# Where a two-layer kernel computes inverse norms and rates: in the preparation instead of at the head of each recurrence piece

## The chip, the cores and the metric

The kernel runs on one core of one Trainium2 chip. The metric is the device time of one execution in microseconds (us). Three runs of the kernel before gave 3310.29, 3290.19 and 3306.56 us, with a median of 3306.56. A core has five engines that each work through their own list of instructions in order: TensorE (PE, matrix products; PEld is its loading of weights), VectorE (DVE), ScalarE (ACT, activation functions), GpSimd (POOL) and SyncE (SP), which here issues the transfers (DMA).

## The reference, cut to what matters

The input is `hidden_states` of shape (16, 512, 256): 16 sequences of 512 tokens with 256 channels, which are 16 heads of 16. Two layers follow, each with an attention part and a feed-forward part; all are residual, with scale and shift from a conditioning vector. The change lies in the attention part of the first layer, whose "fast weights" are a recurrence over chunks of 16 tokens:

```python
q = l2norm(silu(short_conv(h @ Wq.T, cq)).reshape(b, l, H, HD))
k = l2norm(silu(short_conv(h @ Wk.T, ck)).reshape(b, l, H, HD))
v =        silu(short_conv(h @ Wv.T, cv)).reshape(b, l, H, HD)
lr = softplus(h @ Wlr.T + BASE_LR).reshape(b, l, H, 2)
# per chunk: scores of k and q with W_in (4 x 16 per head), softmaxes,
# outer products with v and k that update W_in and W_out, outputs o_t
o = layernorm over the 16 channels of a head; o * (h @ Wg.T) @ Wo.T
```

`l2norm` divides each head's 16 channels by their Euclidean norm, so for every token and head one number, the inverse norm, has to be found for q and one for k. `lr` holds two rates per token and head. The first layer's feed-forward part is a low-rank one with gelu; the second layer has attention over a window of 64 tokens plus four global ones, and a channel mix with gates. The window attention adds masks to its scores.

## The kernel before, in words

**Units.** The sequences are split in two halves of eight, and the tokens in eight blocks of 64. One half and one block make a unit; there are 16. Each unit goes through five streams, written as Python generators: `prepare` (projections, convolution and silu of q, k and v; gate), `chain` (the recurrence), `mlp`, `attend` (window attention), and `mix`. `timetable` (L1111) gives each stream's steps times in units, and the loop at L1126 records the steps of all units sorted by these times. A scheduler then orders each engine's instructions by its own estimate of when each becomes ready. Units of the same half follow one another in the recurrence; units of different halves are independent, so two recurrence chains run side by side.

**Two layouts.** `prepare` has channels on partitions (128 of the 256 channels in each of two tiles, 512 columns = 8 sequences x 64 tokens). The recurrence has sequence and head on partitions (8 x 16 = 128) and, in a piece of 32 tokens, 16 channels x 32 tokens in a row. Between them the data go through device memory: `prepare` writes q, k, v and lr (L422, L461), and `load_piece` (L553) reads a piece back in the other layout (L559, L561). A unit has two pieces (`NPC` = 2), a piece two chunks.

**What is done at the head of a piece.** `load_piece` loads k, v, q and lr into buffers of which each half has one. It then makes the rates: ACT adds 0.001 (L562) and takes the three steps of `log_sigmoid_tail` (L201 to L203), DVE puts them together (L565). For k and then q, ACT squares the 128x512 piece (L550, into one of five buffers shared with the big products), DVE sums the 16 channels (`ss`, L571), ACT takes the inverse root as exp(-0.5 ln x) (L196, L197), and POOL multiplies the piece (L573). ACT then copies a chunk into `tok` with tokens ahead of channels (L589), and DVE makes the first scores from it (L519, L520).

**What is done at the end of a piece.** `finish_piece` (L657) takes the layer norm over a head's channels: mean (L665), squares `osq` (L550), their sum `ov` (L670), its inverse root (L196, L197), product (L673); the result is stored (L674). It works in q's buffer, so the next piece's q can be loaded only after that store.

**Buffers of the preparation.** `t2k("a", ...)` gives 128x512 fp32 buffers from a ring of three (`RING`, L118): `y` (a silu result), `lrT`, `gsb`. `bank` gives one of three banks of the matmuls' accumulator memory (L111), which the streams share. silu needs another function table than ln and exp; `run` (L213) keeps its activations together between two table loads.

**Masks.** All 12 masks (three kinds of block, two parities, two orientations; 128 columns each, bf16) lie on chip, and `add_mask` (L859) adds two of them to a bank by a matmul with the identity (L862). Kinds 0, 1 and 2 belong to blocks 0, 1 and all later ones.

Of the kernel before, what the change touches and what calls it, by code (L numbers as in the profile page):

```python
# [10 lines left out]
F32 = mybir.dt.float32  # L11
# [57 lines left out]
def parity_scales():  # L69

    ch = np.arange(P)
    even = (ch // D) % 2 == 0
    s = 1.0 / math.sqrt(D)
    group, slot = ch // 32, ch % 32
    part = slot // NS < NPART
    sel = -((slot[:, None] % NS == np.arange(NS)[None, :]) & part[:, None]).astype(np.float32)
    k2, pair, _ = np.unravel_index(np.arange(32), (2, 4, NGLOB))  # L80
    selg = np.stack(
        [(group[:, None] == pair) & (slot[:, None] % NS == 2 * k2 + e) & part[:, None] for e in range(2)], 1
    ).astype(np.float32)
    ones_g = np.tile(np.arange(8)[None, :] == (4 * k2 + pair)[:, None], (NR, 1))
    parts = [
        np.stack([even * s, ~even * s, even, ~even], 1),
        group[:, None] == np.arange(4)[None, :],
        sel,
        -selg.reshape(P, -1),
        ones_g,  # L90
    ]
    return np.ascontiguousarray(np.concatenate([p.astype(np.float32) for p in parts], 1))

# [2 lines left out]
def adaln_blocks(ctx: ExitStack, tc: tile.TileContext, a: dict, out: bass.AP):  # L96
# [18 lines left out]
        return ps_a.tile([P, 512], F32, tag="abank", name=name)  # L115


    RING = dict(a=3, b=3, c=6, d=2)  # L118

    def t2k(stream, name, shape=None):  # L120
        return work.tile(shape or [P, 512], F32, tag=f"t2k_{stream}", name=name, bufs=RING[stream])
# [51 lines left out]
    mu = plain("mu", [P, 2, 2])  # L173
    mu1 = ctile([P, 2, 2], "mu1")
    nc.vector.tensor_scalar(mu1, mu, -1.0, 1.0, mul, add)
    marks = plain("parity", [P, 8 + NS + 2 * 32 + 8])
    parity, rowgrp = marks[:, :4], marks[:, 4:8]
    ones_g = marks[:, 72 + NS :]
    ones = ctile([P, 32], "ones")
    nc.vector.memset(ones, 1.0)  # L180
    ones_bf = const.tile([NPART, P], BF16, tag="ones_bf", name="ones_bf")
# [1 line left out]
    sel_bf = const.tile([P, NS + 64], BF16, tag="sel_bf", name="sel_bf")  # L183
    nc.vector.tensor_copy(sel_bf, marks[:, 8 : 72 + NS])
    sel, selg = sel_bf[:, :NS], sel_bf[:, NS:].rearrange("p (n k) -> p n k", n=2)
    masks = const.tile([P, 12, P], BF16, tag="masks", name="masks")
    ident_bf = const.tile([P, P], BF16, tag="ident_bf", name="ident_bf")
    nc.vector.tensor_copy(ident_bf, ident)

# [49 lines left out]
    with tc.tile_pool(name="mod", bufs=1) as mp:  # L239
        masks_f = mp.tile([P, 12, P], F32, tag="masks_f", name="masks_f")  # L240
        nc.sync.dma_start(masks_f, a["masks"].rearrange("p (n k) -> p n k", n=12))
        nc.vector.tensor_copy(masks, masks_f)
        b2_row = mp.tile([1, C], F32, tag="b2_row", name="b2_row")
        nc.sync.dma_start(b2_row, a["V2b"][RANK:])
        b2_parts = mp.tile([1, NPART, C], BF16, tag="b2_parts", name="b2_parts")
# [157 lines left out]
    def prepare(u):  # L403
# [3 lines left out]
        for pc in range(NPC):  # L407
            for n in "qkvo":
                spill(f"{n}{u}_{pc}", [HB, H, D, PT])
            spill(f"lr{u}_{pc}", [HB, H, 2, PT])  # L410
        x = load_x(u, f"xa{u}", "xa", 1)
        hT = hidden("a", f"hTa{u}")
        yield from norm_T(x, 0, 0, b0, f"a{u}", hT)
# [3 lines left out]
        for k in range(2):  # L417
            nc.tensor.matmul(pp[: 2 * H, :], lhsT=w_lr[:, k, :], rhs=hf[k], start=k == 0, stop=k == 1)
        lrT = t2k("a", f"lrT{u}", [P, HB, TB])[: 2 * H]
        nc.scalar.copy(lrT.rearrange("p b t -> p (b t)"), pp[: 2 * H, :])  # L420
        for pc in range(NPC):
            nc.sync.dma_start(  # L422
                spilled[f"lr{u}_{pc}"].rearrange("b h j t -> (h j) b t"),
                lrT[:, :, pc * PT : (pc + 1) * PT],
            )

        for n in range(3):
            ys, convs = [], []
# [30 lines left out]
            for k2, (y, _) in enumerate(ys):  # L459
                for pc in range(NPC):  # L460
                    nc.sync.dma_start(  # L461
                        spilled[f"{'qkv'[n]}{u}_{pc}"][:, k2 * H // 2 : (k2 + 1) * H // 2].rearrange(
                            "b h d t -> (h d) b t"
                        ),
                        y[:, :, pc * PT : (pc + 1) * PT],
                    )
            yield

# [84 lines left out]
    def load_piece(u, pc):  # L553
        half = place(u)[0]
        tag = f"{u}_{pc}"
        s = {}
        for n in "kvq":
            s[n] = rec.tile([P, D, PT], F32, tag=f"dt_{n}_{half}", name=f"dt_{n}{tag}", bufs=1)
            nc.sync.dma_start(s[n], spilled[f"{n}{u}_{pc}"].rearrange("b h d t -> (b h) d t"))  # L559
        lr = rec.tile([P, 2, PT], F32, tag=f"lr_{half}", name=f"lr{tag}", bufs=1)  # L560
        nc.sync.dma_start(lr, spilled[f"lr{u}_{pc}"].rearrange("b h j t -> (b h) j t"))  # L561
        nc.scalar.activation(lr, lr, AF.Copy, bias=0.001)  # L562
        tmp = small(half, f"lrt{tag}", 2 * PT).rearrange("p (j t) -> p j t", j=2)
        log_sigmoid_tail(lr, tmp)
        nc.vector.scalar_tensor_tensor(lr, lr, 0.0, tmp, ALU.max, add)  # L565
        s["lr"] = lr
        s["sum"] = small(half, f"qs{tag}", PT)
        for n in "kq":
            sq = squares(half, s[n], f"sq_{n}{tag}")
            ss = small(half, f"ss_{n}{tag}", PT)  # L570
            nc.vector.tensor_reduce(ss, sq, AX.X, add)  # L571
            inverse_root(ss)
            nc.gpsimd.tensor_tensor(s[n], s[n], over_d(ss), mul)  # L573
        return s


# [185 lines left out]
    def window_attention(i, x):  # L762
# [94 lines left out]
            return keys[:, k2, r, 2 * e : 2 * e + 2].rearrange("p s t -> p (s t)")  # L857

        def add_mask(dst, query_first):  # L859
            at = 2 * min(tb, 2) + (0 if query_first else 6)  # L860
            m = masks[:, at : at + 2].unsqueeze(1).to_broadcast([P, 2, 2, P])
            nc.tensor.matmul(dst, lhsT=ident_bf, rhs=m, start=False, stop=True, skip_group_check=True)  # L862

# [1 line left out]
            nc.tensor.matmul(dst, lhsT=lhsT, rhs=rhs, start=start, stop=False, skip_group_check=True)  # L865

        slots = [(s, s // 2, s % 2) for s in range(NS)]
        queries = lambda r: lambda k2, e: qs[:, k2, 2 * r + e].rearrange("p h t -> p (h t)")

        def find_maxima(r):  # L870
# [313 lines left out]
```

## Time and profile before

| | PE | DVE | ACT | POOL |
|---|---|---|---|---|
| busy, us | 2424.1 | 2396.2 | 1762.1 | 1669.3 |
| share of the span | 73% | 73% | 53% | 51% |
| instructions | 16784 | 4513 | 3738 | 1575 |

The profiled execution took 3303.97 us, and its span from first to last instruction is 3302.2 us. The granted TensorE clock was 0.78 on average. Transfers moved 186.42 MB, 56 GB/s over the span.

Instructions that the change touches, each with its count and the mean of one:

| line, engine | what | count | mean, ns |
|---|---|---|---|
| L550 ACT | squares of k, of q | 32, 32 | 1073, 1069 |
| L571 DVE | sums ss_k, ss_q | 32, 32 | 681, 680 |
| L565 DVE | rates put together | 32 | 376 |
| L573 POOL | k, q times inverse norm | 32, 32 | 1270, 1268 |
| L418 PE | rates projected, 32 columns by 512 | 64 | 739 |
| L862 PE | masks added | 512 | 447, 431 |

A row of the profile reads: line, engine, operation, output<-inputs by the program's names, shapes and count, then busy time, the mean of one, and the idle time of the engine just before, with what ended it. In the views ordered by time a row begins with start and duration in us, and ends, in brackets, with the idle time before it and its releaser. A row that stands for several instructions ends with x and their number. In the busy table by stage the columns are the stretch, its length, busy time (and instructions) of PE, PEld, DVE, ACT and POOL, the granted clock, the busy share of the DMA engines and GB/s. "Share of the chain" is the share of the chain of waits that ended last.

### The profile page before, as it was taken

How to read it: one execution, taken by the hardware profiler on the slowest of the kernel's cores; microseconds unless marked ns; L12 is line 12 of the kernel's file. 1: busy time of each engine (PE TensorE's matmuls, PEld its weight loads, DVE VectorE, ACT ScalarE, POOL GpSimd, SP SyncE). 2: the span in 40 equal slices, each digit the busy share in tenths (PEclk: the TensorE clock that was granted, in tenths of full speed). 3: DMA queues.
4: the chain of work that ended last, by engine and by line, in shares of the span. 5: the costliest groups of instructions: out<-in, count | busy, mean ns of one | idle time of the engine just before them, and what ended most of it. 6: DMA issues, size and time to landing. Idle time of an engine off the chain costs nothing.

```text
span 3302.2 us, 46348 instructions
## 1 busy us (share of the span) xinstructions
PE 2424.1 (73%) x16784; PEld 1461.5 (44%) x16784; DVE 2396.2 (73%) x4513; ACT 1762.1 (53%) x3738; POOL 1669.3 (51%) x1575
## 2 busy tenths in 40 slices
PE   3541255777787878788887878788797878878886
PEld 2210123444444445454554445454454455545564
DVE  1678787868887787788778877877878877774221
ACT  1662354556655656565655656565665645444443
POOL 0245555556566655545546555555556556543112
PEclk7675576878787877878778788788878786869887
DMA  5321112032314131231304122131403121212010
GB/s 149 78 62 19 45 40 67 24 72 56 81 33 96 30 83 46 59 78 43 81 21 100 30 70 67 43 88 37 91 17 95 28 71 34 59 35 58 15 29 27
DMA packets 439305, 186.42 MB, mean 56 GB/s; under 512 B 323937, under 2 KB 413090, under 8 KB 439074
## 3 DMA queue, kind: packets, MB, share of 16 engines
q1 hardware_dynamic: 439074, 183.44, 22.8%
q8 instruction: 132, 2.16, 0.3%
q14 instruction: 99, 0.81, 0.1%
HBM read 116.66 MB, written 66.72 MB: 56 GB/s over the span
## 4 chain that ended last, share of the span: by engine, by line
DVE 32%; PE 28%; POOL 18%; ACT 11%; issue 7%; DMA 3%; SPq 1%; POOLq 0%; DVEq 0%; ACTq 0%
POOL pd_o L526 4%; POOL pd_i L526 4%; DVE pd_kv L623 4%; DVE pp L452 3%; DVE sc_v L519 3%; PE ph L728 3%; PE py L865 3%; PE st L865 2%; PE pz L865 2%; DVE sv L520 2%; PE pproj L994 2%; POOL pd_kv L526 2%; DVE mx L881 2%; DVE do L628 2%; PE pka L1031 2%
## 5 line engine op out<-in xcount | busy, mean ns | idle before, releaser
L526 POOL TENSOR_TENSOR pd_o<-e_k,dt_v 128x1024 f32<-128x1024 f32 x128 | 299.0, 2343 | 234.4 <-DVE e_k L541 234.2
L865 PE MATMUL st<-qs,keys 32*128 32x128 f32 x2048 | 234.3, 351 | 107.2 <-DVE mx L881 47.8
L526 POOL TENSOR_TENSOR pd_i<-e_v,dt_k 128x1024 f32<-128x1024 f32 x128 | 297.3, 2354 | 21.4 <-DVE e_v L541 21.1
L865 PEld LDWEIGHTS st<-qs,keys 32*128 32x128 f32 x2048 | 199.5, 240 | 163.0 <-DVE mx L881 61.5
L653 POOL TENSOR_TENSOR pd_kv<-hid,pd_kv 128x1024 f32<-128x1024 f32 x64 | 150.7, 2354 | 188.8 <-DVE fw L624 183.1
L628 DVE TENSOR_REDUCE do<-pd_o 128x64 f32<-128x1024 f32 x126 | 152.5, 1214 | 100.3 <-POOL pd_o L526 100.3
L628 DVE TENSOR_REDUCE di<-pd_i 128x64 f32<-128x1024 f32 x128 | 155.3, 1213 | 85.7 <-POOL pd_i L526 85.7
L865 PE MATMUL sc<-keys,qs 32*128 32x128 f32 x2048 | 169.5, 321 | 63.0 <-DVE mx L881 43.4
L700 PE MATMUL pwo<-w_WoT,oT 128*128 128x256 f32 x256 | 103.1, 560 | 142.6 <-POOL oT L693 140.7
L865 PEld LDWEIGHTS sc<-keys,qs 32*128 32x128 f32 x2048 | 134.6, 210 | 129.8 <-DVE mx L881 63.4
L881 DVE TENSOR_REDUCE mx<-sc 128x4 f32<-128x512 f32 x256 | 168.4, 679 | 19.0 <-PE sc L862 19.0
L623 DVE TENSOR_TENSOR_SCAN pd_kv<-within,pd_kv 128x1024 f32<-128x1024 bf16 x64 | 176.5, 2758 | 1.0
L526 POOL TENSOR_TENSOR pd_kv<-hid,dt_v 128x1024 f32<-128x1024 f32 x64 | 150.1, 2345 | 45.9 <-DVE hid L615 41.0
L519 DVE TENSOR_TENSOR sc_k<-tok,fw 128x1024 f32<-128x1024 f32 x128 | 155.5, 1215 | 16.0 <-ACT tok L589 14.6
L994 PE MATMUL pproj<-w_proj,yT 128*128 128x256 f32 x512 | 136.7, 411 | 36.7 <-DVE yT L972 33.7
L217 ACT ACT_TABLE_LOAD x110 | 141.1, 1283 | 19.7 <-PE pQ L735 18.1
L519 DVE TENSOR_TENSOR sc_v<-tok,fw 128x1024 f32<-128x1024 f32 x128 | 150.4, 1215 | 1.4
L865 PE MATMUL py<-pT,values 128*32 128x128 f32 x2048 | 130.4, 374 | 26.8 <-ACT pT L918 26.3
L520 DVE TENSOR_REDUCE sv<-sc_v 128x64 f32<-128x1024 f32 x128 | 149.7, 1210 | 0.0
L972 DVE TENSOR_TENSOR yT<-py,rs 128x256 f32<-128x256 f32 x128 | 51.5, 415 | 133.8 <-ACT rs L968 133.7
L918 ACT ACTIVATE pT<-st 128x512 f32<-128x512 f32 x256 | 135.4, 615 | 22.0 <-PE st L862 21.8
L865 PE MATMUL py<-pg,vglob 32*32 32x128 f32 x1536 | 71.8, 342 | 99.1 <-ACT pg L929 99.1
(244 smaller groups left out, 6821.5 us busy)
## 6 DMA issues: line engine op xcount, KB each, us to landing
values<-values SPq DMA_DIRECT2D x56, 256.0 KB
gate_a<-gates SPq DMA_DIRECT2D x64, 128.0 KB
xa<-in_x_dram SPq DMA_DIRECT2D x32, 256.0 KB
x<-in_x_dram SPq DMA_DIRECT2D x32, 256.0 KB
gate_c<-gates SPq DMA_DIRECT2D x64, 128.0 KB
gate_d<-gates SPq DMA_DIRECT2D x64, 128.0 KB
q<-y SPq DMA_DIRECT2D x64, 128.0 KB
dt_q<-q SPq DMA_DIRECT2D x32, 256.0 KB
```

Source lines behind the costliest of these rows:

```text
L217: ins = nc.scalar.activation(*args[0], **args[1])
L519: engine.tensor_tensor(pr, tok.unsqueeze(1).to_broadcast(every), w.unsqueeze(2).to_broadcast(every), mul)
L520: nc.vector.tensor_reduce(dst, pr, AX.X, add)
L526: engine.tensor_tensor(pr, hid.unsqueeze(2).to_broadcast(every), tok.unsqueeze(1).to_broadcast(every), mul)
L623: nc.vector.tensor_tensor_scan(flat, within, flat, 0.0, mul, add)
L628: nc.vector.tensor_reduce(t, pr, AX.X, add)
L653: nc.gpsimd.tensor_tensor(po, qh.unsqueeze(2).to_broadcast([P, R, D, CH]), upto, mul)
L700: nc.tensor.matmul(po[:, n * C : (n + 1) * C], lhsT=pair(oT, k, 2 * b2 + n), rhs=w_o[:, k, :], start=k == 0, stop=k == 1,)
L865: nc.tensor.matmul(dst, lhsT=lhsT, rhs=rhs, start=start, stop=False, skip_group_check=True)
L881: nc.vector.tensor_reduce(mx[:, j], sc[j].rearrange("p (s k) -> p s k", s=NS), AX.X, ALU.max)
L918: nc.scalar.activation(pT[j], st[j], AF.Exp)
L994: nc.tensor.matmul(po[:, n * C : (n + 1) * C], lhsT=yT[:, k2, par].rearrange("p e t -> p (e t)"), rhs=w_proj[:, k2, par, :], start=k2 == 0 ...
```

## The change

The inverse norms and the rates are made by `prepare`, with channels on partitions, once per unit:

- For q and k, after silu, ACT squares the two `y` tiles, and PE sums each head's 16 channels with a matmul against `by_head`, a matrix of ones and zeros of 32 columns that comes with the constants (heads 0 to 7 in the first 8 columns, repeated). The two results go to partitions 0 to 31 and 32 to 63 of one bank, `pn`. ACT takes Ln and Exp of 64x512, and two stores write the 8 useful rows of each part to device memory as `rn`.
- The rates take their softplus on 32x512 before they are stored, once per unit instead of once per 32 tokens with 128x64.
- `load_piece` loads lr and rn (one buffer each per half) and multiplies k and q with rn on POOL, as before. Its squares, sums, roots and softplus are gone.
- The preparation's ring of 128x512 buffers has four instead of three.
- All 12 masks are converted once and stored in device memory. On chip are the four of one kind; `window_attention` loads them, in two transfers, at the first three blocks of the first half.

```diff
-    RING = dict(a=3, b=3, c=6, d=2)
+    RING = dict(a=4, b=3, c=6, d=2)
...
-    masks = const.tile([P, 12, P], BF16, tag="masks", name="masks")
+    masks = const.tile([P, 4, P], BF16, tag="masks", name="masks")
+    all_masks = dram.tile([P, 12, P], BF16, tag="all_masks", name="all_masks")
...
-        nc.vector.tensor_copy(masks, masks_f)
+        masks_b = mp.tile([P, 12, P], BF16, tag="masks_b", name="masks_b")
+        nc.vector.tensor_copy(masks_b, masks_f)
+        nc.sync.dma_start(all_masks, masks_b)
...
-        nc.scalar.copy(lrT.rearrange("p b t -> p (b t)"), pp[: 2 * H, :])
-        for pc in range(NPC):
-            nc.sync.dma_start(
-                spilled[f"lr{u}_{pc}"].rearrange("b h j t -> (h j) b t"),
-                lrT[:, :, pc * PT : (pc + 1) * PT],
-            )
+        lrf = lrT.rearrange("p b t -> p (b t)")
+        nc.scalar.activation(lrf, pp[: 2 * H, :], AF.Copy, bias=0.001)
+        tmp = t2k("a", f"lrt{u}")[: 2 * H]
+        log_sigmoid_tail(lrf, tmp)
+        nc.vector.scalar_tensor_tensor(lrf, lrf, 0.0, tmp, ALU.max, add)
+        nc.sync.dma_start(spilled[f"lr{u}"].rearrange("b h j t -> (h j) b t"), lrT)
...
+            if n < 2:
+                pn = bank(f"pn{u}_{n}")
+                for k2, (y, _) in enumerate(ys):
+                    sq = t2k("a", f"sq{u}_{n}_{k2}")
+                    nc.scalar.activation(sq, y.rearrange("p b t -> p (b t)"), AF.Square)
+                    nc.tensor.matmul(
+                        pn[32 * k2 : 32 * (k2 + 1)], lhsT=by_head, rhs=sq, start=True, stop=True, skip_group_check=True
+                    )
+                rn = t2k("a", f"rn{u}_{n}", [P, HB, TB])
+                rf = rn.rearrange("p b t -> p (b t)")[:64]
+                nc.scalar.activation(rf, pn[:64], AF.Ln)
+                nc.scalar.activation(rf, rf, AF.Exp, scale=-0.5)
+                for k2 in range(2):
+                    nc.sync.dma_start(
+                        spilled[f"rn{u}"][:, k2 * H // 2 : (k2 + 1) * H // 2, n].rearrange("b h t -> h b t"),
+                        rn[32 * k2 : 32 * k2 + H // 2],
+                    )
...
-        lr = rec.tile([P, 2, PT], F32, tag=f"lr_{half}", name=f"lr{tag}", bufs=1)
-        nc.sync.dma_start(lr, spilled[f"lr{u}_{pc}"].rearrange("b h j t -> (b h) j t"))
-        nc.scalar.activation(lr, lr, AF.Copy, bias=0.001)
-        tmp = small(half, f"lrt{tag}", 2 * PT).rearrange("p (j t) -> p j t", j=2)
-        log_sigmoid_tail(lr, tmp)
-        nc.vector.scalar_tensor_tensor(lr, lr, 0.0, tmp, ALU.max, add)
-        s["lr"] = lr
+        for n in ("lr", "rn"):
+            s[n] = rec.tile([P, 2, PT], F32, tag=f"{n}_{half}", name=f"{n}{tag}", bufs=1)
+            nc.sync.dma_start(
+                s[n], spilled[f"{n}{u}"][:, :, :, pc * PT : (pc + 1) * PT].rearrange("b h j t -> (b h) j t")
+            )
         s["sum"] = small(half, f"qs{tag}", PT)
-        for n in "kq":
-            sq = squares(half, s[n], f"sq_{n}{tag}")
-            ss = small(half, f"ss_{n}{tag}", PT)
-            nc.vector.tensor_reduce(ss, sq, AX.X, add)
-            inverse_root(ss)
-            nc.gpsimd.tensor_tensor(s[n], s[n], over_d(ss), mul)
+        for j, n in ((1, "k"), (0, "q")):
+            nc.gpsimd.tensor_tensor(s[n], s[n], over_d(s["rn"][:, j]), mul)
...
-            at = 2 * min(tb, 2) + (0 if query_first else 6)
+            at = 0 if query_first else 2
...
+        if tb < 3 and half == 0:
+            kind = 2 * min(tb, 2)
+            for n in range(2):
+                nc.sync.dma_start(masks[:, 2 * n : 2 * n + 2], all_masks[:, 6 * n + kind : 6 * n + kind + 2])
```

More of the change, by code (lines that the diff above doesn't have):

```diff
@@ L90, in parity_scales @@
         ones_g,
+        (ch // D)[:, None] == np.arange(32)[None, :] % 8,
     ]
@@ L175, in adaln_blocks @@
     nc.vector.tensor_scalar(mu1, mu, -1.0, 1.0, mul, add)
-    marks = plain("parity", [P, 8 + NS + 2 * 32 + 8])
+    marks = plain("parity", [P, 8 + NS + 2 * 32 + 8 + 32])
     parity, rowgrp = marks[:, :4], marks[:, 4:8]
-    ones_g = marks[:, 72 + NS :]
+    ones_g = marks[:, 72 + NS : 80 + NS]
+    by_head = marks[:, 80 + NS :]
     ones = ctile([P, 32], "ones")
@@ L409, in prepare @@
                 spill(f"{n}{u}_{pc}", [HB, H, D, PT])
-            spill(f"lr{u}_{pc}", [HB, H, 2, PT])
+        spill(f"lr{u}", [HB, H, 2, TB])
+        spill(f"rn{u}", [HB, H, 2, TB])
         x = load_x(u, f"xa{u}", "xa", 1)
```

## The prediction

> **What bounds the kernel now.** I read the page's first and fourth parts for a saturated engine, then a steady stretch of the per-stage busy table, then VectorE's order of time across one moment at which both recurrence chains change their piece, the spot the change rewrites.
>
> ```profile
> PE 2424.1 (73%) x16784; PEld 1461.5 (44%) x16784; DVE 2396.2 (73%) x4513; ACT 1762.1 (53%) x3738; POOL 1669.3 (51%) x1575
> DVE 32%; PE 28%; POOL 18%; ACT 11%; issue 7%; DMA 3%; SPq 1%; POOLq 0%; DVEq 0%; ACTq 0%
> ```
> ```profile
> 1000.00:2500.00 1500.00, 1214.19 (x8514) 734.46 (x8513) 1202.83 (x2251) 882.27 (x1869) 827.51 (x778) 0.80 0.25 60
> ```
>
> Nothing is saturated. In the steady 1500 us PE and DVE are each busy 80 to 81%, and the chain of work that ended last hops: 32% DVE, 28% PE, 18% POOL. What binds is dependent work on in-order engines: two recurrence chains (one per half of the batch) in lockstep, held now and then by the attention's matmuls. The squares of the layer norm at a piece's end (L550, osq) recur in pairs, at 1416.4, 1600.9, 1798.1 and 1985.6 us: a period of some 187 us. There are 32 pieces, of which 30 change in 15 pairs; these 15 boundaries are where the change acts.
>
> ```profile
> 1598.56 0.28 DVE L541 SCALAR_TENSOR_TENSOR e_k<-e_k,lr,fw 128x64 f32<-128x64 f32 x1
> ...
> 1601.98 0.69 DVE L670 TENSOR_REDUCE ov<-osq 128x32 f32<-128x512 f32 x1 [3.14 <-ACT osq L550]
> ...
> 1618.00 0.68 DVE L571 TENSOR_REDUCE ss_q<-sq_q 128x32 f32<-128x512 f32 x1
> ...
> 1621.25 1.22 DVE L519 TENSOR_TENSOR sc_q<-tok,fw 128x1024 f32<-128x1024 f32 x1 [0.78 <-ACT tok L589]
> 1622.39 0.68 DVE L571 TENSOR_REDUCE ss_k<-sq_k 128x32 f32<-128x512 f32 x1
> ...
> 1627.14 0.69 DVE L571 TENSOR_REDUCE ss_q<-sq_q 128x32 f32<-128x512 f32 x1 [0.47 <-ACT ss_k L197]
> ...
> 1632.19 1.22 DVE L519 TENSOR_TENSOR sc_q<-tok,fw 128x1024 f32<-128x1024 f32 x1 [0.51 <-ACT tok L589]
> ```
>
> A boundary: the old piece's last rate-weighted exponentials at 1598.56, its layer norm, then the new pieces' norms, and the second chain's first query scores only at 1632.19. In these 36 us DVE works 27.0 and ACT 28.5. GpSimd, which makes the outer products, begins one at 1600.35 and the next at 1643.56.
>
> **What the Trainium skill says.** "Perfetto Trace Analysis", Sequencer Loop: an engine's instruction waits in its own queue for its semaphores, so what stands behind it waits too. The trace agrees: ov above waits 3.14 us for osq, whose input was ready before and which stood on ACT behind a copy (qs) that waited for the attention's pq. "TensorE: Matmul & The Clock Gate", Measured speedup vs the span model: matmuls in different column tiles run together (2.38 times for three of M=32, N=512). The trace agrees in kind: the 256 half-width records of pQ last 632 ns each but 90.7 us together, 354 ns apiece. "ScalarE: Activation LUTs", Table sets: ln and exp share a set, so the added Ln and Exp need no switch; the present L196 and L197 run back to back in the trace without a table load.
>
> **The change part by part.** The profiled execution took 3303.97 us, 1.8 over its 3302.2 span; the median of the runs is 2.6 above it, which I add at the end.
>
> 1. *Work taken from the boundary.* Per piece ACT loses sq_k 1.07, sq_q 1.07, four roots of 0.23 and four steps of lr of 0.26: 4.1 us. DVE loses ss_k 0.68, ss_q 0.68 and the lr step, 0.37: 1.7 us, 55 over 32 pieces. GpSimd keeps its two products (1.27 each), now fed by the load of rn. Lower bound of the gain: in the chain of waits from 1595 to 1640 us the removed instructions hold 4.9 us. Upper: after the first ov DVE idles 5.5 us in that boundary, mostly for these producers, and loses 3.2 us of work between 1600 and 1633, 8.7; and the built order puts the first new key scores ahead of ov, into the 3.1 us hole, 11.8. I take 7.5: the late queries (written out, read back at 1611.2, then 1.27 + 0.64 before scores) stay serial and become next in line. 15 x 7.5 = -112; bounds -177 and -74.
>
> 2. *PE.* Per unit four fp32 matmuls of 32 columns by 512, two records each: 16 x 8 = 128 records. plr, of the same shape, takes 593 ns a record: 76 us if serial, 38 if the two column tiles overlap fully; at pQ's 354 it is 45. PE is on the chain for 28% of 3302 = 925 us of 2424 busy, 38%. So +17, bounds +15 and +29.
>
> 3. *ACT in the preparation.* Four squares at 0.60 (y's row), two pairs Ln and Exp at 0.60 + 0.65 (rs's rows), three more passes over the rates at 0.57 (lrT's row): 2.4 + 2.5 + 1.7 = 6.6 us a unit, 105 in all. ACT's chain share is 11% x 3302 / 1762 = 21%: +22, between +10 if it fills idle ACT and +40. DVE gains one pass over the rates (32x512) a unit, some 0.70 us (sg's row of 512 columns, 0.68): 11 x 44% = +5 (+2 to +11).
>
> 4. *The new wait.* Ln waits for pn on PE; behind it on ACT stand the chains' exponentials and tok copies, for which DVE and GpSimd wait. lrT waits for plr 39.1 us in 16, 2.4 each; 32 of those are 77 us. Where PE is late anyway it is already in step 2; I add +8 (0 to +25).
>
> 5. *DMA and buffers.* Issues on SP rise from 1047 to 1134, 87 x 0.34 = 30 us of a queue that idles mostly: nothing added, because each rn store stands ahead of v's stores (L461) and the loads (L559) that need it come a period later; were that cover gone, one store and one load, about 2.6 us each as for dt_k's first load (issued 102.25, landed 104.83), would join a boundary. The mask store, 0.39 MB, goes before wm's second load, which waits for PE until 36.6 anyway: zero. Two reloads of masks for new kinds: at most 2 x 2.6, taken +3 (0 to +5). The fourth t2k_a buffer and the five big products no longer shared with squares: nothing, since no wait in the list of waits is put down to them.
>
> 6. *Start.* In the first preparation nothing runs beside it: PE's k projections now queue behind pn, which needs Silu of q. +5 (0 to +10); the 5 us or so of removed sq, ss and roots there offset part of it.
>
> Sum: -112 + 17 + 22 + 5 + 8 + 0 + 3 + 5 = -52, giving 3252 for the profiled execution and **3255** for the median. All best ends together: -177 + 27 = -150, 3157. All worst: -74 + 120 = +46, 3353.
>
> **The rivals.**
> - *Late PE swallows it* (chance 22%). The gain is real at the boundary, but attention's matmuls, 81% busy, are then what the next yT, mx or qs waits for. For it: the stretch before 1600.9 is pproj, pq, pk, pq on the chain. Against: DVE holds more of the chain. Gain 4.9 x 15 = 74, the additions of 60, and 15 more of waiting: 3304 - 74 + 75 = 3305, so 3308 (3290 to 3330).
> - *ACT now waits in the wrong place, slower* (12%). In the built order of the changed kernel, at most steady boundaries Ln of the keys' rn stands ahead of the second chain's ov root. pn stands on PE behind pproj, which needs yT. From e_k: outer products 4.7, their sum 1.2, yT 0.8, pproj 3.8, pn 1.4, Ln and Exp 1.1 make 13 us until that root, which now ends 6 us after e_k: 7 us later each time. The price is 15 x 7 = 105, in place of step 4's 8: 3252 - 8 + 105 = 3349, so 3352. It decides once the stand exceeds 60 / 15 = 4 us a period. Against it: the loads have slack until the other chain's scores are done.
> - *The whole boundary shrinks* (16%). DVE's holes close and the additions fall into idle time: 3157 to 3215, say 3190.
>
> **Chances.** The forecast has 50% (3215 to 3290). A measurement of this kernel can tell about 1%, 33 us, from no change. Below 3273 lie the whole third rival and some 44 points of the forecast: 60% faster. Within 1% lie the rest of the forecast and the first rival: 28%. The second rival is above 3340: 12% slower. The range, 3180 to 3335, leaves out the second rival and the far end of the third.
>
> **What would show it.** Right: osq to the second chain's hid, 36.7 us at 1600.9 (1637.6), some 7 shorter; the waits of dt_k and dt_q's products for ss (59.0 and 31.1 us) gone; DVE busy about 45 us less; period near 180. Step 2: pn's busy time near 45 us. Step 4: Ln of rn waiting for pn under 2.4 us each. Wrong: the same period with longer waits of ov's root or tok (second rival), or of mx, yT and qs for PE (first).

## The result, and the profile after

The changed kernel takes 3339.49 us (median of 4 runs, 3336.37 to 3343.70) against 3304.07 us of the kernel before in the same comparison: a ratio of 1.0111, 95% interval 1.0094 to 1.0128. It is slower by 1.1%. The forecast was 3255 us, the range 3180 to 3335, and faster at 60%. It was wrong in sign. Medians and ratios here and below use fast runs alone; of all the runs only one, of e15 (3187 us), was slow.

The page of the changed kernel, its busy totals and its chain of waits:

```profile
PE 2437.6 (73%) x16912; PEld 1436.5 (43%) x16912; DVE 2361.0 (71%) x4433; ACT 1756.3 (53%) x3596; POOL 1697.7 (51%) x1575
...
PE 5%; DVE 2%; POOL 2%; ACT 1%; issue 1%; DMA 0%; POOLq 0%; SPq 0%; ACTq 0%; DVEq 0%
```

DVE has lost 35 us of work (2396.2 before) and ACT 6; PE has gained 13 and POOL, with as many instructions, 28. These totals alone don't explain 35 us more. The chain adds up to a tenth of the span: the trace of this run loses it early, and it isn't read here.

The same 1500 us of the busy table by stage, the same columns:

```profile
1000.00:2500.00 1500.00, 1206.72 (x8405) 712.85 (x8401) 1171.57 (x2173) 864.72 (x1776) 838.13 (x758) 0.80 0.25 59
```

PE got through 8405 matmuls in this stretch where it was 8514 before, and took 80% of it as before.

The place in time says more than the totals. These are the starts of the layer norm's squares (osq, the first of each pair), read from the two traces, and the periods between them:

```
boundary      1      4      6       7       8       9      10      11      12      16
before    351.9  870.5 1231.3  1416.4  1600.9  1798.1  1985.6  2173.5  2358.6  3021.0
after     353.8  869.5 1228.3  1422.8  1613.3  1804.0  1995.4  2186.5  2377.6  3057.0
ahead by   -1.9   +1.0   +3.0    -6.4   -12.4    -5.9    -9.8   -13.0   -19.0   -36.0
```

Up to 1228 us the changed kernel is within 4 us and in the end ahead, although it starts 5 us later (212.1 against 206.7). From there to boundary 13 every period is some 191 us long (190.4 to 191.4; the first of them 194.6), where before it was 184.5 to 187.9 with one of 197.2. The periods after 13 lose another 13 us, most of it in the first of them (183.4 against 174.7). The boundary itself isn't longer. DVE in order of time at a boundary of the changed kernel (osq at 2186.5), to be held against the lines of 1598.56 to 1632.19 in the prediction:

```profile
2188.46 1.27 DVE L691 TENSOR_REDUCE ov<-osq 128x32 f32<-128x512 f32 x2
...
2202.36 2.34 DVE L460 SCALAR_TENSOR_TENSOR pp<-xp,w_cv,pp 128x512 f32<-128x512 f32 x3 [5.45 <-ACT pp L458]
2207.42 1.22 DVE L546 TENSOR_TENSOR sc_q<-tok,fw 128x1024 f32<-128x1024 f32 x1 [2.73 <-ACT tok L610]
...
2214.20 1.21 DVE L546 TENSOR_TENSOR sc_q<-tok,fw 128x1024 f32<-128x1024 f32 x1
...
2220.45 0.28 DVE L625 TENSOR_TENSOR hid<-scs,fw 128x128 f32<-128x128 f32 x1
```

The sums ss are gone and the second chain's hid starts 33.9 us after osq; before, the median of the five steady boundaries was 34.6. DVE stands idle instead: 5.45 us for ACT, 2.73 for tok. ACT at the same boundary:

```profile
2186.55 1.94 ACT L577 ACTIVATE osq<-dt_q 128x512 f32<-128x512 f32 x2
...
2190.12 0.23 ACT L202 ACTIVATE ov<-ov 128x32 f32<-128x32 f32 x1
2190.26 0.62 ACT L610 COPY tok<-dt_v 128x256 f32<-128x256 f32 x1
2192.42 0.59 ACT L487 ACTIVATE rn<-pn 64x512 f32<-64x512 f32 x1 [1.54 <-PE pn L482]
2193.05 0.63 ACT L488 ACTIVATE rn<-rn 64x512 f32<-64x512 f32 x1
2193.58 0.21 ACT L201 ACTIVATE ov<-ov 128x32 f32<-128x32 f32 x1
2193.82 0.23 ACT L202 ACTIVATE ov<-ov 128x32 f32<-128x32 f32 x1
...
2206.76 0.63 ACT L610 COPY tok<-dt_q 128x256 f32<-128x256 f32 x1 [0.82 <-POOL dt_q L594]
```

This is the order that the second rival named: the keys' Ln waits for pn and stands ahead of the second chain's ov root, which ends 7.5 us after osq began; before, it was 3.8:

```profile
2173.47 1.96 ACT L550 ACTIVATE osq<-dt_q 128x512 f32<-128x512 f32 x2
...
2176.88 0.35 ACT L197 ACTIVATE ov<-ov 128x32 f32<-128x32 f32 x2
```

In the built order the keys' Ln stands just ahead of the two osq at boundary 7 and between the ov roots at 8 to 13, the stretch in which most of the loss runs up (9.5 us of it come earlier, between boundaries 6 and 7). That made it the first theory (A) to be tested. Theory B was the first rival (PE's added work), theory C that any change of the built order moves the time by about as much.

The largest of PE's waits in the changed kernel is a new one, for the squares ahead of pn (us in all, times, the longest):

```profile
PE pn L482 <- ACT sq L481: 130.0, 16, 17.1
```

The prediction has it in the first preparation alone (step 6). All 16 end before 1420 us, and 125 us of them before 1050, where the two kernels are level, so this wait isn't what makes the later periods long.

### The profile page after: what moved, and what is told of

The parts are those of the page before. It is cut to its first block, busy times and chain, and to the rows that moved or that the text cites. A ratio compares the mean times of both kernels' runs of the same rounds, so it can differ in the third digit from the quotient of the medians.

```text
span 3334.3 us, 46592 instructions
## 1 busy us (share of the span) xinstructions
PE 2437.6 (73%) x16912; PEld 1436.5 (43%) x16912; DVE 2361.0 (71%) x4433; ACT 1756.3 (53%) x3596; POOL 1697.7 (51%) x1575
## 5 line engine op out<-in xcount | busy, mean ns | idle before, releaser
L886 PE MATMUL st<-qs,keys 32*128 32x128 f32 x2048 | 207.9, 347 | 85.9 <-DVE yT L998 39.9
L886 PEld LDWEIGHTS st<-qs,keys 32*128 32x128 f32 x2048 | 175.0, 235 | 146.9 <-DVE mx L907 50.5
L907 DVE TENSOR_REDUCE mx<-sc 128x4 f32<-128x512 f32 x256 | 167.5, 677 | 34.9 <-PE sc L883 34.8
L886 PEld LDWEIGHTS sc<-keys,qs 32*128 32x128 f32 x2048 | 141.7, 218 | 111.8 <-DVE mx L907 52.7
L482 PE MATMUL pn<-sq,c_parity 128*32 128x512 f32 x128 | 60.8, 865 | 130.9 <-ACT sq L481 130.0
L886 PE MATMUL py<-pT,values 128*32 128x128 f32 x2048 | 122.5, 355 | 28.5 <-ACT pT L944 27.9
L749 PE MATMUL ph<-PT,w_v 64*128 64x512 f32 x256 | 125.6, 822 | 22.5 <-ACT z L222 18.9
```

The lines of the kernel that those rows point to most:

```text
L749: nc.tensor.matmul(ph, lhsT=w_v1[rows, f // 2, :], rhs=pT[rows], start=True, stop=True)
L907: nc.vector.tensor_reduce(mx[:, j], sc[j].rearrange("p (s k) -> p s k", s=NS), AX.X, ALU.max)
```

## The experiments

Times are medians of the runs of one comparison; ratios are to the kernel before in the same comparison, with their 95% intervals.

### The parts by themselves

Kernel before with one part of the change put in:

```diff
-    masks = const.tile([P, 12, P], BF16, ...)      # e8: masks and ring alone
+    masks = const.tile([P, 4, P], BF16, ...)
...
-        nc.scalar.copy(lrT..., pp[: 2 * H, :])     # e4: masks and rates
+        nc.scalar.activation(lrf, pp[: 2 * H, :], AF.Copy, bias=0.001)
+        log_sigmoid_tail(lrf, tmp)
...
-            sq = squares(half, s[n], ...)          # e3: masks and norms
+                nc.tensor.matmul(pn[...], lhsT=by_head, rhs=sq, ...)
+                nc.scalar.activation(rf, pn[:64], AF.Ln)
```

> The change's third part alone: masks of one kind on chip, written out once and loaded again for the first kinds, and four buffers in the preparation's ring in place of three; rates and norms as before. The built order on ACT is that of the kernel before. All theories: +3 for two reloads, 3300 to 3312; theory C as well, since the order stays.

> The change's rates and masks without its norms: squares, sums and roots of keys and queries stay in the piece. Theory A and theory B: nothing of pn or rn in it; four ACT steps of 0.26 and one DVE step of 0.37 leave each piece and 1.7 us of ACT a unit come, so 3290 to 3310. Theory C: may leave that by 20 us or more.

> The change's norms and masks without its rates: the load of lr and the softplus of the rates stay in the piece as before. At boundaries 8 and 9 of the built order the keys' rn stands before or between the osq pair, at 10 and later behind both ov roots. Theory A: with rn no longer between the ov roots most of the loss is gone, 3300 to 3315. Theory B: pn is all there, so 3335 to 3345. Theory C: no telling.

Measured: masks 3301.73 us (0.9999, 0.9986 to 1.0012), rates 3314.07 (1.0039, 1.0027 to 1.0051), norms 3312.59 (1.0026, 1.0011 to 1.0041). The masks cost nothing. Rates and norms each cost a little, 0.65% together, and the whole change 1.11%: the parts don't add up. The norms alone, with the keys' rn behind the ov roots at most steady boundaries, cost 10 us and not 35, as theory A has it; the rates are 4 us above their expectation.

### The place of the keys' Ln

First by the timetable, in both kernels:

```diff
-        yield prepare, [(12, u - 1.7, u - 0.7)]
+        yield prepare, [(12, u - 1.8, u - 0.8)]
```

> The changed kernel with its preparation placed a tenth of a unit earlier in the timetable (u - 1.8 to u - 0.8 in place of u - 1.7 to u - 0.7), nothing else. In the built order the Ln and Exp of the keys' inverse norms (rn) then stand ahead of the osq pair on ACT and no longer between the two pieces' ov roots. Theory A (rn in the wrong place at the boundary): the 36 us lost from the seventh boundary on come back, 3339 - 36 = about 3303 or lower, and the period from 1230 us on is 187 us or less in place of 190.5 to 191.4. Theory B (PE's added pn work and late PE swallow the gain): the place of rn does not matter, 3339 within 10 us, the period stays near 191. Theory C (any change of the built order moves the time by some 1%): no telling, between 3290 and 3370, and the kernel before moves as much under the same shift.

> Control: the kernel before with the same shift of its preparation (u - 1.8 to u - 0.8), nothing else. Theory A: there is no rn in it, so the shift is worth little, 3304 within 10 us. Theory B: the same, 3304 within 10. Theory C: moves by 20 us or more in either direction, since the built order changes on every engine.

Measured: 3384.0 us (1.0255, 1.0216 to 1.0295) and 3334.97 (1.0107, 1.0069 to 1.0146). Theory A's number fell, but the tool was too coarse: the shift alone costs the kernel before 32 us, and the changed kernel so shifted also loads function tables 256 times in place of 224. That is theory C's case, and a warning for what follows: a move that touches none of the work costs as much as the whole change did.

Then by moving only the steps in dispute, emitted two of the preparation's steps later (e5 for the keys, e6 for both):

```diff
         for n in range(3):
             for k2 in range(2):
+                if held and k2 == 1:
+                    norms(*held.pop())      # pn, Ln, Exp and the stores
...
-                pn = bank(f"pn{u}_{n}")     # and the rest of it
+                if n in (1,):
+                    held.append((n, sqs))
```

> The changed kernel with the matmul pn, the Ln and Exp and the stores of the keys' inverse norms emitted two of the preparation's steps later (between the two values projections); squares, queries' norms, rates and masks unchanged, the timetable too. In the built order of the steady boundaries the keys' Ln then stands behind all ov roots and the tok_v copies on ACT, as it does not in the changed kernel. Theory A (the keys' Ln ahead of the second chain's ov root costs the steady periods their 3 to 4 us each): 36 us come back, 3303 or lower, steady period 187 or less. Theory B (PE's added work swallows the gain): 3339 within 10 us. Theory C (what the built order as a whole happens to be decides): anywhere from 3290 to 3360, and the place of the keys' Ln tells nothing by itself.

> As the run before, but the queries' pn, Ln, Exp and stores too are emitted two steps later (between the two projections of the keys). In the built order the keys' Ln stands behind the ov roots, the tok_v copies and oT. Theory A: as the run before, 3303 or lower. Theory B: 3339 within 10. Theory C: may differ from the run before by 20 us or more though only the queries' norms moved, which lie nowhere near the boundary.

Measured: 3294.31 us (0.9981, 0.9969 to 0.9992) and 3293.07 (0.9970, 0.9958 to 0.9982). The same work in another place takes 43 us off the changed kernel (1.0111 / 0.9981 = 1.0130, of 3303) and makes it a little faster than the kernel before. Theory B falls as far as it means the amount of PE's work: PE does all of it here. ACT of e5 at a boundary, in order of time:

```profile
2160.37 1.96 ACT L586 ACTIVATE osq<-dt_q 128x512 f32<-128x512 f32 x2
...
2164.59 0.22 ACT L202 ACTIVATE ov<-ov 128x32 f32<-128x32 f32 x1
...
2167.09 0.22 ACT L202 ACTIVATE ov<-ov 128x32 f32<-128x32 f32 x1
2167.22 2.36 ACT L862 COPY values<-pvv 64x512 f32<-64x512 f32 x4
2170.73 0.59 ACT L443 ACTIVATE rn<-pn 64x512 f32<-64x512 f32 x1 [1.15 <-PE pn L438]
```

The keys' Ln is behind both roots. But the second root is hardly earlier for it: it ends 6.9 us after osq began (2167.09 + 0.22), in the changed kernel 7.5 (2193.82 + 0.23). Moving the Ln helps; that it helps through the ov root isn't shown.

### The work left out

e7 leaves out the matmul pn (the sum over the channels; Ln reads the squares themselves), e9 all that the change adds to the preparation.

```diff
-                    nc.tensor.matmul(pn[32 * k2 : 32 * (k2 + 1)], lhsT=by_head, rhs=sq, ...)   # e7
-                nc.scalar.activation(rf, pn[:64], AF.Ln)
+                nc.scalar.activation(rf, sq[:64], AF.Ln, bias=1.0)
...
-        log_sigmoid_tail(lrf, tmp)                 # e9, with sq, pn, Ln and Exp
+        nc.scalar.activation(lrf, pp[: 2 * H, :], AF.Square)
```

> The changed kernel with the matmul pn left out, and so the sum over a head's channels: Ln reads the first 64 rows of the second square directly, with 1 added (the values of the norms are then others; the squares, Ln, Exp, stores and loads stay). Theory A: rn waits for PE no more and stands ahead of the osq pair in the built order, so 3300 or lower. Theory B: PE loses 61 us of busy time, 38% of it on the path: 3339 - 23 = 3316, within 8. Theory C: open, 3290 to 3360.

> The changed kernel with its additions left out: no squares, no pn, no Ln and Exp of rn, no softplus of the rates in the preparation; a square of the rates' projection stands in for both the rates and the norms (so these values are others), with one store each, and the pieces load and multiply as in the changed kernel. What is left is the prediction's first step, the work taken from the boundary, by itself. Theory D (the boundary was never as short as step 1 had it: after the removed work, the queries' product dt_q is next, behind the load of oT on SP and the products of oT on GpSimd): 2 to 3 us a boundary and the ACT passes off, 3304 - 35 = 3260 to 3280. Theory E (step 1 was right and the additions ate it): 3304 - 112 + 3 = about 3195, below 3230 in any case.

Measured: 3290.85 us (0.9959, 0.9944 to 0.9973) and 3289.87 (0.9979, 0.9958 to 0.9999). This is the ladder that the prediction's sum needed. With nothing added, taking the work from the boundary is worth 7 us by the ratio and 13 by the medians. ACT's additions, put back, cost 1 us by the medians (e7), and PE's another 2 to 3 (e6, e5); by the ratios e7 is even below e9, and e5 level with it. Each rung has a built order of its own, so such differences are too small to be read as prices. Put back where the change has them, the same additions cost 44 us by the ratio and 50 by the medians. Theory E, that step 1 was right and the additions ate it, is out by 95 us. Theory D's size, 3260 to 3280, is not reached either.

### The next step in line at the boundary

In e5 the queries' product waits its turn on GpSimd, in order of time:

```profile
2167.39 1.27 POOL L703 TENSOR_TENSOR dt_q<-dt_q,ov 128x512 f32<-128x512 f32 x1 [1.17 <-ACT ov L202]
...
2175.07 2.49 POOL L723 TENSOR_TENSOR oT<-oT,gT 128x512 f32<-128x512 f32 x2 [2.11 <-ACT oT L720]
...
2177.70 1.26 POOL L603 TENSOR_TENSOR dt_q<-dt_q,rn 128x512 f32<-128x512 f32 x1
```

oT is written out, loaded back and multiplied ahead of it. So the branch that begins with oT was put a tenth of a unit later, in e5, in the changed kernel and in the one before:

```diff
-        yield mlp, [(10, u + 2, u + 2.65)]
+        yield mlp, [(10, u + 2.1, u + 2.65)]
```

> The kernel with the keys' norm deferred (the run labelled e5) with the low-rank branch, which begins with the load and products of oT, placed a tenth of a unit later (u + 2.1 to u + 2.65 in place of u + 2 to u + 2.65), nothing else. In the built order of the steady boundaries both products dt_q<-dt_q,rn then stand ahead of oT's on GpSimd, and both loads of dt_q ahead of oT's on SP. Theory D: the second hid comes 2 to 4 us sooner, 15 x 3 = 45 off, 3294 - 45 = 3250, 3235 to 3275. Theory E: oT lies elsewhere than on the path, 3294 within 10. Theory C (chance of the built order): anything from 3250 to 3340.

> The changed kernel with the same later low-rank branch, nothing else. In the built order the keys' Ln then stands behind the ov roots and the tok_v copies, but still ahead of the tok_q copies and the qs, and both dt_q products ahead of oT. Theories A and D: most of both gains, 3250 to 3290. Theory E: only the 36 us of the keys' Ln, 3303 within 10. Theory C: anything from 3250 to 3340.

> Control: the kernel before with the same later low-rank branch, nothing else. In its built order the first dt_q product then stands ahead of oT on GpSimd, the second behind it. Theory D: with the squares, sums and roots still in the boundary oT is not what is last, 3304 within 12. If the later branch is worth its time by itself, whatever the change does, 3250 to 3280.

Measured: 3279.72 us (0.9941, 0.9920 to 0.9962), 3280.61 (0.9942, 0.9919 to 0.9964) and 3300.03 (1.0004, 0.9992 to 1.0016). Two versions of the change now beat both kernels, and the control doesn't move. The reason isn't theory D's, though. Medians over the five periods between boundaries 8 and 13, from osq, read from the traces; the middle column is the difference of the other two:

```
                      osq to second hid   second hid to next osq   period
before                      34.6                 152.9             187.5
after                       34.1                 157.0             191.1
e5 keys' norm deferred      32.2                 152.5             184.7
e9 additions left out       32.0                 162.5             194.5
e10 e5, mlp late            38.4                 145.0             183.4
e11 after, mlp late         38.6                 147.6             186.2
e12 before, mlp late        31.2                 156.5             187.7
```

In e12 the boundary is 3.4 us shorter than before and the rest 3.6 longer; in e10 it is 3.8 longer and the rest 7.9 shorter. The changed kernel's loss too lies wholly after the second hid. How long the boundary is doesn't tell how long the period is. (One run of each kernel was profiled. Those of e9, e11 and e12 lie at or near the long end of their runs: 3311 of 3278 to 3311, 3291 of 3277 to 3291, and 3310 of 3294 to 3313.)

### Is the boundary on the path at all?

e13 leaves out the layer norm at a piece's end, e14 half of the contraction of pka, pr, pkv and pgate, e15 both, all in the kernel before:

```diff
-        nc.gpsimd.tensor_tensor(o, o, over_d(mean), sub)     # e13: with mean, osq, ov,
-        sq = squares(half, o, f"osq{tag}")                   # root and product
...
-            for k in range(2):                               # e14
+            for k in range(1):
```

> The kernel before with the layer norm at a piece's end left out (mean, osq, ov, its root and the two products on GpSimd of every piece; the output is stored as it is): the boundary's serial path loses 4.9 us at least (osq's start at 2173.6 to the store of o at 2178.5) and the engines lose per piece 2.5 us of GpSimd, 1.5 of DVE and some 2.0 of ACT. Theory F (the boundary is on the path of the steady period, as the prediction's step 1 had it): 15 x 5 to 10, so 3304 - 75 to 150 = 3154 to 3229. Theory G (PE and what other streams hold in order set the period; what a boundary gains is waited off later in it): 3304 within 25.

> The kernel before with half of the contraction left out of four products that no recurrence reads (pka, pr and pkv of the channel mix and pgate): half of 76.7 + 67.0 + 63.3 + 80.3 us of PE's busy time, 144 us, 9 a period; nothing is taken from a boundary. Theory F: PE has 20% idle in a steady period and the recurrence does not wait for these, 3304 within 25. Theory G: at PE's share of the chain, 38%, 3304 - 55 = 3249, and down to 3180 if PE alone sets the period.

> The kernel before with both left out, the layer norm at the piece's end and half of the contraction of pka, pr, pkv and pgate. Theory F: as e13, 3154 to 3229. Theory G: as e14, some 3249. If the two hold each other (either alone is waited off at the other): well below the sum of the two gains measured alone.

Measured: 3244.84 us (0.9822, 0.9806 to 0.9839), 3264.17 (0.9888, 0.9871 to 0.9905) and 3158.71 (0.9539, 0.9491 to 0.9586; three runs, from 3130 to 3160). Off 3303 that is 58, 39 and 144 us, 152 by the last ratio. Neither F nor G holds alone: e13 and e14 each miss the numbers of both, and the two together give 144 where the two gains add up to 97. The reading that fits is that boundary and PE hold each other, so that what is taken from one is in part waited off at the other. It isn't the only one left: each build has its own order, and a shift of order alone moved the kernel before by 32 us (e2), where the excess here is 47. The prediction's way of costing, an engine's busy time by its share of the chain, has no place for such an excess.

### Another Ln at an ov root

e16 puts e6 and the later branch together; in its built order the queries' Ln comes between the two osq and the first chain's ov roots.

> The changed kernel with both norms' matmul, Ln, Exp and stores deferred by two steps (as e6) and the low-rank branch a tenth of a unit later (as e10 and e11). In its built order the steady boundaries have the queries' Ln between the two osq and the first chain's ov roots. If a Ln that waits for PE ahead of an ov root costs 3 us a period wherever it stands: 3280 + 40 = 3320. If the later branch alone is what counts: 3280 within 10.

Measured: 3280.86 us (0.9933, 0.9918 to 0.9949), as e10 and e11. In its trace the queries' Ln doesn't itself wait at these boundaries (0.02 us idle before it); a copy ahead of it, xp, waits 3 to 5 us for PE's pp. The second chain's root ends 15 to 16 us after the first osq began (7.5 in the changed kernel) and the second hid starts 44 us after it, and still the kernel is faster than the one before. So a late root doesn't by itself cost the period; theory A as the second rival had it, 7 us at the root each time, doesn't hold in general.

### What differs in the steady periods

The busy table by stage over the five periods between boundaries 8 and 13, of the changed kernel, then of e5:

```profile
1613.30:2568.80 955.50, 787.28 (x5590) 470.86 (x5590) 744.32 (x1386) 547.57 (x1127) 537.61 (x480) 0.79 0.25 59
```
```profile
1600.90:2527.30 926.40, 749.64 (x5596) 452.51 (x5594) 743.11 (x1387) 551.36 (x1129) 524.53 (x481) 0.82 0.26 61
```

The same number of instructions on every engine within 6, and DVE and ACT as busy (POOL 2.6 us a period less in e5). Over the whole span the loads of function tables don't differ either, 224 and 222. PE takes 787.28 us for 5590 matmuls in one and 749.64 for 5596 in the other, 7.5 us a period more, at a granted clock of 0.79 against 0.82; its idle time is 33.6 and 35.4 us a period. The period differs by 5.8. Six-microsecond stretches of the changed kernel show the clock at half speed while PE works:

```profile
2259.00:2265.00 6.00, 5.24 (x36) 4.58 (x38) 5.81 (x16) 0.31 (x1) 3.19 (x3) 0.50 0.00 0
2265.00:2271.00 6.00, 4.48 (x16) 2.68 (x15) 3.79 (x6) 2.14 (x5) 5.71 (x8) 0.50 0.00 0
2271.00:2277.00 6.00, 5.25 (x23) 1.84 (x22) 5.79 (x9) 5.59 (x16) 1.74 (x1) 0.50 0.17 47
```

where PE was busy 75 to 87% of 18 us; and of e5, after almost 12 busy us at 0.60 and 0.55 (2238 to 2250), the full clock:

```profile
2250.00:2256.00 6.00, 6.00 (x24) 2.42 (x26) 5.55 (x14) 4.16 (x9) 3.01 (x2) 1.00 0.00 0
2256.00:2262.00 6.00, 6.00 (x21) 2.32 (x21) 5.74 (x9) 5.88 (x12) 1.66 (x1) 1.00 0.01 3
```

The Trainium skill says in "TensorE: Matmul & The Clock Gate", Part 1, that PE's clock runs at half rate by default and that sustained activity releases it. The trace agrees as far as 0.50 and 1.00 go: its record of the clock has these two values alone. A record of pn takes 593 ns where the whole of it lies at full clock and 1061 where it lies at half (medians of 39 and 55 records in the changed kernel).

So PE's busy time can be split by the clock it ran at. Per period over the same five, in us, with the time at half clock counted half in the third column:

```
                         busy   of it at half clock   half x 0.5 + full   idle   period
before                   154.3          64.7                121.9          34.7    189.0
after                    157.5          68.7                123.1          33.6    191.1
e1 after, prepare early  153.9          61.1                123.4          40.2    194.2
e5 keys' norm deferred   149.9          56.3                121.8          35.4    185.3
e10 e5, mlp late         146.6          47.9                122.6          37.3    183.9
e12 before, mlp late     147.7          51.2                122.1          39.5    187.2
```

PE's work at full speed is nearly the same in all of them. Of the 7.5 us that PE is busier in the changed kernel than in e5, half of 12.4, or 6.2, come from more of the work falling into half clock. That explains PE's time; it doesn't yet explain the period. Against the kernel before, e12 has 6.6 us less of busy time and a period only 1.8 shorter, because PE waits longer; and e1, with the longest period, has less of its work at half clock than the kernel before. The mean clock doesn't show this, since it counts PE's idle time too: e12 has 0.79, like the changed kernel.

```profile
1620.60:2556.40 935.80, 738.54 (x5552) 463.47 (x5551) 740.05 (x1410) 561.82 (x1181) 530.30 (x480) 0.79 0.26 60
```

If PE's waits decide when its clock falls, the built order sets the speed of the matmuls behind them. Whether that is a cause of the long periods was tried by filling PE's gaps ahead of two norms' transposes with matmuls whose result is overwritten, in both kernels:

```diff
             pt = bank(f"pt_{tag}_{r2}")
+            if tag[0] in "ab":
+                for _ in range(6):
+                    nc.tensor.matmul(pt, lhsT=ident_bf, rhs=ident_bf..., start=True, stop=True)
```

> The kernel before with six matmuls of 128x128 by 512 columns (bf16) added ahead of each group of transposes of the norms of two streams (pt_a, pt_b), into the bank that the transposes then overwrite: 384 in all, some 0.43 us each by the mask rows of the profile, 165 us more for PE, in place where it waits 84 us for xn_a and xn_b. Theory H (the granted clock follows PE's gaps and sets the period): the clock in the steady periods rises by 0.01 or more above 0.80 and the time stays within 15 us of 3303 or falls, in spite of the work. Theory I (the clock only goes with the period): the clock may rise, but the added work costs 38% of what does not fit the gaps, (165 - 84) x 0.38 = 31 us or more: 3330 or longer.

> The changed kernel with the same six matmuls ahead of the transposes of pt_a and pt_b, where its PE waits 130 us in all. In its built order the keys' Ln stands ahead of the osq pair and no longer between the ov roots. Theory H: the clock in the steady periods rises above 0.79 and the period falls below 191 us, 3339 - 10 or lower. Theory I: 3339 + (165 - 130) x 0.38 = 3352 or longer. Theory A (the place of the keys' Ln alone): 3303 plus the same 13, 3316.

Measured: 3319.83 us (1.0058, 1.0042 to 1.0073) and 3266.92 (0.9896, 0.9865 to 0.9926). The first is 16 us longer by the medians, just outside theory H's 15 and short of theory I's 3330. The second goes H's way, and much further than any of the three numbers. The changed kernel with 384 useless matmuls is the fastest that still does all the work: 1.0% below the kernel before and 2.1% below the change as it came (0.9896 / 1.0111 = 0.9787). Its five steady periods:

```profile
1595.10:2508.50 913.40, 754.93 (x5707) 444.04 (x5706) 729.64 (x1378) 545.60 (x1125) 527.80 (x478) 0.83 0.26 62
```

and those of e17, then of the kernel before:

```profile
1599.00:2544.90 945.90, 768.52 (x5666) 462.86 (x5667) 749.62 (x1406) 550.19 (x1171) 527.52 (x478) 0.81 0.25 59
1600.90:2546.10 945.20, 771.52 (x5551) 465.94 (x5550) 760.71 (x1410) 554.68 (x1174) 511.69 (x480) 0.80 0.25 59
```

In e18 PE does 117 matmuls more and is busy 32 us less than in the changed kernel, at 0.83. The added rows of pt_a and pt_b held 105 us of the whole span (192 at 423 ns, 192 at 394), and PE's total is 2428.0 us, below the 2437.6 without them. But the built order moved as well (the keys' Ln is ahead of the osq pair), and in the kernel before, with the same filling, the clock of the whole profiled run rose from 0.780 to 0.789 and the time by 16 us, all of it after boundary 13: its steady periods hold 115 matmuls more in the same time. That the filled gaps and not the new order made e18 fast isn't shown; that PE can do more matmuls in less busy time is.

## Why the prediction was wrong

**What was right.** The masks (step 5, +3): e8 measured nothing. The start (step 6, +5): the first osq is 5.4 us later, though at boundary 1 only 1.9 are left. The removed waits of dt_k and dt_q for ss are gone, DVE is 35 us less busy (about 45 forecast), and the wait of rn's Ln for pn (step 4) is 20.5 us in 12, 1.7 each against the 2.4 taken. pn's busy time (step 2) is 60.8 us, inside its bounds of 38 and 76 but above the 45 taken: the 593 ns that the step worked from is a record at full clock, and pn's mean is 865.

**Step 1, the boundary, -112, failed.** Alone, with nothing added, it measured 7 to 13 us in the one order that was built (e9). Two assumptions in it failed. From osq to the second hid the boundary became 0.5 us shorter in the changed kernel and about 2.5 in e5 and e9, not 7.5. The step had named the serial path of the queries as next in line, and the waits agree: POOL's products of dt_q and dt_k, which waited 31.1 and 59.0 us for ss, now wait 46.6 and 13.1 for their loads; that this path alone holds the boundary isn't shown. And a boundary that is shorter by 15 x 3 us isn't a kernel that is shorter by 45: in e12 the rest of the period grew by what the boundary lost.

**Steps 2 to 4, +52, had a number that came near by luck.** Where the change puts the additions they cost 44 to 50 us over e9; two steps later (e5, e6) the same work costs 3 to 4 by the medians, and nothing by the ratio for e5. So it isn't the busy time by a share of the chain that was paid: that price knows no place.

**What decided wasn't in the sum.** The built order from the seventh boundary on goes with steady periods that are longer by 3.6 us in the median and 2.1 in the mean; the same instructions with pn, Ln and Exp of the keys two steps later are 43 us faster. The first rival (late PE swallows it) is out by e5 as far as it rests on PE's added work; that PE is late for its clock is open. Its signs are mixed: the wait of mx for PE rose from 19.0 to 34.8 us (e18 has 40.2), and that of qs fell from 40.9 to 12.5. The second rival's signs are there: the wait of the layer norm's product for the ov root rose from 15.9 to 54.2 us (33.0 in e5), and that of sc_q for tok from 23.5 to 54.3, the latter as long in the faster e5, 53.0. That rival had the place (the keys' Ln, ahead of the second ov root), the sign and nearly the size (3352 against 3339), but not the way: the second root ends 3.7 us later than before, not 7; the second hid isn't late for it; the loss comes after it; and in e16 the root is later still at no cost. What in the new order makes PE slower and the rest of the period longer is open: more of PE's work at half clock goes with it, and e17 and e18 don't settle whether that is cause or consequence.

## What to carry to other kernels

Where several in-order engines are each busy four fifths of the time, leave the removed work out first, with nothing put in its place: here that run showed at once that 112 us weren't to be had. It isn't an upper bound, though, since it too has only one built order: e10, e11, e16 and e18 do all the added work and are 9 to 23 us faster than e9. Before believing a loss, move the added instructions a step or two in the order that a scheduler builds; here that was worth 43 us. Compare the time that PE takes for the same matmuls, and how much of it lies at half clock, since a change of order that leaves every count alone can show there.

## What the runs showed of the hardware

PE's busy time for the same 1118 matmuls a period ranged from 146.6 us (e10) to 157.5 (the changed kernel), on a core that ran alone, with 47.9 and 68.7 us of it at half clock; counted at full speed it was 122.6 and 123.1. Half clock stayed through 18 us in which PE was busy 75 to 87%. With 384 matmuls added, PE's total busy time was 10 us lower in one kernel (e18, whose order changed too) and 42 us higher in the other (e17). Over 132 runs of the kernel before, 0.01 of mean granted clock goes with 8 us of time (correlation -0.47).
